# Graph layers on one core: angular nets in slot order, one product for keys and values, source gathers in place, and an earlier search of edges

## The chip, the core and the metric

The kernel runs on one core of a Trainium2 chip. The core has a matrix engine (PE, with its weight loads shown as PEld), a vector engine (DVE), an activation engine (ACT), a general engine (POOL, which here mostly issues gathers and scatters) and SyncE (SP, which issues transfers). The metric is the device time of one execution in microseconds (us), lower is better.

## The reference

A graph of 6250 nodes (128 features) and 206,250 edges, sorted by destination, goes through two layers, each followed by a residual add and a layer norm.

```python
# layer 1: five rounds of normalized neighbour sums, then a product
for _ in range(K):                                   # K = 5
    h = segment_sum(h[col] * w[:, None], row, num_segments=N)
    x_out = x_out + coef * h
y1 = x_out @ weight.T + bias
...
# layer 2: attention over the edges of each destination
def _conv_per_edge(x_src, edge_attr, edge_sh, Wang, Wlin, W1, b1, W2):
    rad = relu(edge_attr @ W1 + b1) @ W2
    g = edge_sh @ Wang.T
    return x_src * g @ Wlin * rad
x_src = node_attr[src]
k = _conv_per_edge(x_src, ..., Wang_k, Wlin_k, W1k, b1k, W2k)    # 64 wide
v = _conv_per_edge(x_src, ..., Wang_v, Wlin_v, W1v, b1v, W2v)    # 128 wide
alpha = einsum('ehq,qk,ehk->eh', q[dst], Wdot, k)                # 8 heads
attn  = softmax of alpha over the edges of one destination
out   = segment_sum(attn[..., None] * v, dst) @ Wout
```

The change is about `x_src * g` for keys and values together, about `relu(edge_attr @ W1 + b1)`, and about the lists of sources and edge attributes that both need.

## The kernel before

The nodes are cut into 49 tiles of 128. Everything runs in three stages.

**The count stage** (`count_rows`) writes `counts`, a matrix that says how often each node is a source of each other node. For tile `t`, `hot` makes two one-hot tables on DVE (L223), `count` multiplies them on PE (L357) and ACT evicts them (L361), and `put` transposes on DVE (L370, L375) and stores from SP. Tiles come in chunks of 7 (the first two chunks are 2 and 5). For each chunk, `look_at` gathers destinations on POOL (L274); `find_of` counts on DVE where each node's edges begin (L283), makes the positions (L288), and gathers the sources `src_e` on POOL (L290, 7 gathers of 128 rows); `split` on DVE takes the sources apart (L311, L313 to L318) for the tables of the chunk. The loop over `t` writes out by hand where each of these stands: in the old text `find_of` and the next `look_at` come when `t + 2 == a - 3`, `split` when `t + 2 == a - 1`, where `a` is the chunk's first tile. PE, DVE, ACT and POOL run in the order written here.

**The propagation** (`propagate`) does the five rounds as dense products. Each round has four quarters of destinations; in each, for 49 source tiles, SP loads `counts`, DVE (L600) and ACT (L605 to L613) cast it, and PE multiplies (L617). After each step over a source tile, `next(side, None)` runs one step of a side job: first `order_nodes`, which ranks the nodes by degree, then `lay_edges`, which lays the edges of each ranked tile out in slots. A tile has as many slots as `WIDTHS` says (64 down to 22, 1658 in all); slot `j` of a tile holds the `j`-th edge of each of its 128 nodes. `lay_edges` goes by pieces of up to 16 slots, five side steps apart. For a piece, `gather` gathers its edge attributes `ea_l` on POOL (L816), and with the first piece of a tile all the tile's sources into `src_all` (L812); two pieces later ACT splits off an upper part (L823), then DVE takes the rest (L827), then DVE transposes both parts into `eT_l`, a ring of 4 buffers (L835), and POOL stores both to `eas_o` (L841). PE, DVE and ACT run in the order written; POOL's order in this stage is chosen by a scheduler.

**The attention stage** (`attend`) goes through the slots in 433 groups of up to 4 (397 have 4). `fetch` gathers on POOL the source's features, one gather a slot (L961), into 6 buffers, and has SP load the edge attributes `ea` as four blocks `b` of 32 edges, each with its slots side by side. In iteration `i` PE runs `nets(i)` (three products of 512 columns, L1005: one for the radial net's first layer into `p_h`, two for keys and values into the two banks of `p_g`), `radial(i - 1)` (L1024), `turn(i + 1)` (transposes of the gathered features, L991) and `keys(i - 1)` (L1038, L1040). ACT makes the relu (L1007), evicts `p_r` (L1028) and the transposes (L994). DVE multiplies the features with both angular nets into `mkv` (L1013, two products a group), then keys and values with the radial part (L1045 to L1049), and between these takes steps of the softmax of the tile before (L1074 to L1121; the long ones are L1090, L1094 and L1097).

In `nets` the columns of a product are ordered (block, slot, edge), since that is how `ea` lies in memory; `r1`, `mkv` and the features are ordered (slot, block, edge), so L1007 and L1013 reorder as they read and write.

Of the kernel before, what the change touches and what calls it, by code (L numbers as in the profile page):

```python
# [12 lines left out]
AF = mybir.ActivationFunctionType  # L13
OP = mybir.AluOpType
# [4 lines left out]
P = 128  # L19
# [24 lines left out]
SC = 16  # L44
# [183 lines left out]
def count_rows(tc, row, first, cnt, dinv, hs, srct, dstt, tab_lo, tab_hi, iota, ident, ident_b,  # L228
# [10 lines left out]
    nc = tc.nc  # L239
    with tc.tile_pool(name="cr1", bufs=1) as one, tc.tile_pool(name="cr2", bufs=2) as two, \  # L240
# [8 lines left out]
        at = one.tile([P, NT], I32, name="at_e")  # L249
# [52 lines left out]
        def scale(t0, t1):  # L302
            for t in range(t0, t1):
                nc.scalar.mul(hs[:, t], hs[:, t], dinv[:, t:t + 1])
# [3 lines left out]
        def split(a, b):  # L308

            x, n = slice(a, b), b - a  # L310
            nc.vector.tensor_tensor(ok[:, :n], iota[:, None, :SLOTS].to_broadcast([P, n, SLOTS]),  # L311
                                    cnt[:, x, None].to_broadcast([P, n, SLOTS]), OP.is_lt)
            nc.vector.tensor_single_scalar(low[:, :n], src[:, x], 63, OP.bitwise_and)  # L313
            nc.vector.tensor_single_scalar(high[:, :n], src[:, x], 6, OP.logical_shift_right)
            nc.vector.tensor_copy(lh[:, x, 0:2], low[:, :n, None, :].to_broadcast([P, n, 2, SLOTS]))

            for i in (2, 3):
                nc.vector.scalar_tensor_tensor(lh[:, x, i], ok[:, :n], -float(P), high[:, :n],  # L318
                                               op0=OP.mult, op1=OP.add)

        def turn(t):

            p_t = pt.tile([P, 2, P], BF, name="p_lh")
            for i in range(2):
                nc.tensor.transpose(p_t[:, i, :], lh[:, t, 2 * i:2 * i + 2].rearrange("p a j -> p (a j)"),
                                    ident_b)
            turned[t] = two.tile([P, 2, 64], BF, name="lhT")
            for a in range(2):
                y = slice(64 * a, 64 * a + 64)
                nc.scalar.copy(turned[t][y], p_t[y, :, y])  # L330

        def hot(t):

            v = turned.pop(t)
            oh_lo = two.tile([P, 64 // Q, 64, Q], BF, name="oh_l")
            one_hot(nc, oh_lo, v[:, 0, :], tab_lo, 64)
            oh_hi = two.tile([P, 64 // Q, 4 * H4, Q], BF, name="oh_h")
            one_hot(nc, oh_hi, v[:, 1, :], tab_hi, 4 * H4)
            return oh_lo, oh_hi
# [61 lines left out]
        def look_at(i):  # L401
            if i < len(chunks):
                look(ends[i], ends[i + 1])

        def find_of(i):
            find(ends[i], ends[i + 1], *chunks[i])

        with tc.manual_schedule(engines=MANUAL | {mybir.EngineType.Pool}):
            look_at(0)
            find_of(0)  # L410
            look_at(1)
            split(*chunks[0])
            hots = {}
            for t in range(-2, NT + 1):
                for i, (a, b) in enumerate(chunks[2:]):
                    if t + 2 == a - 3:
                        find_of(i + 2)
                        look_at(i + 3)
                    if t + 2 == a - 1:
                        split(a, b)  # L420
                if t == 0:
                    hots[1] = hot(1)
                    split(*chunks[1])
                if 0 <= t + 2 < NT:
                    turn(t + 2)
                if 0 <= t + 1 < NT and t != 0:
                    hots[t + 1] = hot(t + 1)
                if t == -1:
                    find_of(1)
                    look_at(2)  # L430
                if 0 <= t < NT:
                    count(t, *hots.pop(t))
                    next(more, None)
                if 0 <= t - 1 < NT:
                    put(t - 1)
                if t == NT - 9:
                    nc.vector.tensor_scalar(dinv, cnt, 1.0, None, OP.add)
                    nc.scalar.activation(dinv, dinv, AF.Sqrt)
                    nc.vector.reciprocal(dinv, dinv)
                if t >= NT - 8:  # L440
                    scale(min(6 * (t - NT + 8), NT), min(6 * (t - NT + 9), NT))
# [358 lines left out]
def lay_edges(tc, one, ring, rows, srct, eat, src_all, eas_o):  # L800

    nc = tc.nc
    at = one.tile([P, WIDTHS[0] // SC, NT], I32, name="at_l")
    for c in range(WIDTHS[0] // SC):
        nc.vector.tensor_scalar(at[:, c], rows[:, :, 1], float(c * SC), None, OP.add)

    def gather(t, c, s, n):  # L810
        if c == 0:
            nc.gpsimd.indirect_dma_start(  # L812
                out=src_all[:, OFFS[t]:OFFS[t + 1]], out_offset=None, in_=srct[:, :],
                in_offset=bass.IndirectOffsetOnAxis(ap=at[:, 0, t:t + 1], axis=0))
        e = ring.tile([P, SC * 32], F32, name="ea_l", bufs=6)[:, :n * 32]
        nc.gpsimd.indirect_dma_start(  # L816
            out=e, out_offset=None, in_=eat[:, :],
            in_offset=bass.IndirectOffsetOnAxis(ap=at[:, c, t:t + 1], axis=0))
        return n, s, e

    def split(n, s, e):
        upper = ring.tile([P, SC * 32], FR, name="up_l", bufs=3)[:, :n * 32]
        nc.scalar.copy(upper, e)  # L823
        return n, s, e, upper

    def rest(n, s, e, upper):
        nc.vector.tensor_sub(e, e, upper)  # L827
        return n, s, e, upper

    def turn(n, s, e, upper):  # L830

        ys = []
        for x in (upper.bitcast(F32), e):
            y = ring.tile([P, SC * 32], F32, name="eT_l", bufs=4)[:, :n * 32]
            nc.vector.transpose(y, x)  # L835
            ys.append(y)
        return n, s, ys

    def put(n, s, ys):
        for i, y in enumerate(ys):  # L840
            nc.gpsimd.dma_start(  # L841
                bass.AP(tensor=eas_o.tensor, offset=eas_o.offset + (i * 32 * OFFS[NT] + s) * P,
                        ap=[[n * 32, 4], [OFFS[NT] * P, 32], [1, n * 32]]), y)

    todo = [(t,) + p for t in range(NT) for p in pieces(t)]
    got = {}
    for p in range(len(todo) + 5):
        for f, late in ((put, 5), (turn, 4), (rest, 3), (split, 2), (gather, 0)):
            if 0 <= p - late < len(todo):
                got[p - late] = f(*(got[p - late] if late else todo[p]))  # L850
        for _ in range(5):
            yield


def pieces(t):

    return [(c, OFFS[t] + c * SC, min(SC, WIDTHS[t] - c * SC)) for c in range(-(-WIDTHS[t] // SC))]
# [30 lines left out]
def attend(tc, w1, b1, wang, w2, wlin, wqd, wout, ident, rows, c_iota, src_all, eas_o, x1_d, x1_r, out):  # L888


    nc = tc.nc
    WM = WIDTHS[0]
    with ExitStack() as s:
# [9 lines left out]
        b1_s = one.tile([P, 1], F32, name="b1_s")  # L903
# [4 lines left out]
        with tc.tile_pool(name="at_w", bufs=1) as pool:  # L908
            wz = pool.tile([P, 2 * D], F32, name="wz")
            nc.vector.memset(wz, 0.0)  # L910
            for src, dst, at in ((w1, w1_s, 0), (wang, wang_s, 64)):
                n = src.shape[1]
# [19 lines left out]
        ea, kv, qw, x1s, keep, ok, al = {}, {}, {}, {}, {}, {}, {}  # L932
        xs, xT, r1, mkv, rr = {}, {}, {}, {}, {}
# [62 lines left out]
        def nets(g):  # L996

            t, j, n = groups[g]

            p_h = pp.tile([P, CH], F32, name="p_h")  # L1000
            p_g = pp.tile([P, 2, CH], F32, name="p_g")
            i = j % SC
            e = ea[t, j // SC][:, :, i * 32:(i + n) * 32]
            for o, wt in ((p_h, w1_s), (p_g[:, 0], wang_s[:, :D]), (p_g[:, 1], wang_s[:, D:])):
                nc.tensor.matmul(o[:, :n * P], wt, e, start=True, stop=True)  # L1005
            r1[g] = two.tile([P, 4, P], F32, name="r1")
            nc.scalar.activation(r1[g][:, :n].rearrange("p j (b e) -> p b j e", b=4),  # L1007
                                 p_h[:, :n * P].rearrange("p (b j e) -> p b j e", b=4, e=32),
                                 AF.Relu, bias=b1_s)
            mkv[g] = two.tile([P, 2, 4, P], F32, name="mkv")  # L1010
            x = xT.pop(g)[:, :n].rearrange("p j (b e) -> p b j e", b=4)
            for i in range(2):
                nc.vector.tensor_tensor(  # L1013
                    mkv[g][:, i, :n].rearrange("p j (b e) -> p b j e", b=4),
                    p_g[:, i, :n * P].rearrange("p (b j e) -> p b j e", b=4, e=32), x, OP.mult)

        def radial(g):

# [114 lines left out]
        with tc.manual_schedule(engines=MANUAL):  # L1133
            for i in range(-3, len(groups) + 1):
# [11 lines left out]
                if live[0]:  # L1146
                    keys(i - 1)
                    t, j, n = groups[i - 1]
# [162 lines left out]
def gnn_kernel(ctx, tc, x, srcf, dstx, srcp, dstp, easT, eas, wT0, b0, wq, wdot, w1, b1,  # L1311
# [40 lines left out]
    with ExitStack() as s:  # L1352
# [44 lines left out]
        def loads():  # L1397
# [5 lines left out]
            for e in range(0, EP, SUP * CH):  # L1403
                yield
                nc.scalar.dma_start(eat[e:e + SUP * CH], eas[e:e + SUP * CH], cond=unsorted < 1)

        count_rows(tc, row, first, cnt, dinv, hs, srct, dstt, tab_lo, tab_hi, iota, ident,
                   ident_b, counts, loads())

# [101 lines left out]
```

## Time and profile before

| what | us |
|---|---|
| median of 3 runs (4299.01 to 4313.89) | 4309.51 |
| the profiled execution, its own time | 4312.55 |
| its span, first to last instruction | 4310.8 |
| PE busy in the span | 3753.0 (87%) |
| DVE busy | 3492.5 (81%) |
| POOL busy | 2418.2 (56%) |
| ACT busy | 2052.8 (48%) |
| window 65 to 505 us (count): PE, DVE, POOL busy | 357, 401, 132 |
| window 525 to 2060 us (propagation): PE, DVE, POOL busy | 1450, 1100, 539 |
| window 2060 to 4311 us (attention): PE, DVE, POOL busy | 1938, 1961, 1718 |

A line of a group names the source line, the engine, the operation, output and input tiles, the count, then the busy time and the mean duration of one in ns, then the idle time of the engine just before these instructions with what ended it. In a timeline a line begins with its start and its duration in us, and the bracket at its end is the idle time before it. A wait line reads: who waited for whom, the total in us, how many times, and the longest. Shares over the whole span mix three stages with different limits, so stages are read one by one.

### The profile page before, as it was taken

The numbers are of one execution on the slowest core, as the hardware profiler recorded it, in microseconds if no ns is written. First come the engines' busy times: TensorE is split into PE (matmuls) and PEld (weight loads), VectorE is DVE, ScalarE is ACT, GpSimd is POOL, SyncE is SP. The second block draws the span as 40 slices with busy tenths as digits, with TensorE's granted clock in tenths as the row PEclk, the third lists the DMA queues.
The fourth block names the chain that finished last, engine by engine and source line by source line (L and its number), as shares of the span: only waits on it lengthen the run. The fifth ranks groups of instructions, "written<-read, shape, count | busy, mean of one in ns | idle before, by whom it ended". The sixth has DMA issues, their size and how long they took to land.

```text
span 4310.8 us, 76970 instructions
## 1 busy us (share of the span) xinstructions
PE 3753.0 (87%) x26392; PEld 3321.9 (77%) x26392; DVE 3492.5 (81%) x6175; ACT 2052.8 (48%) x4187; POOL 2418.2 (56%) x2388
## 2 busy tenths in 40 slices
PE   4877799799999999997788888888888888888883
PEld 3777688587878888875778888788888788887883
DVE  5999795587777877665598889998889989989995
ACT  3777754464654655543334444444434443444441
POOL 4233006633334433122777777777777777777776
PEclk8676699899999999998899999999999999999996
DMA  3776556699988998563655555556555655654551
GB/s 109 200 192 172 130 143 155 158 235 224 230 205 214 246 237 227 155 165 99 122 100 99 107 100 100 105 97 106 98 99 104 111 100 98 108 103 95 102 106 44
DMA packets 394939, 603.48 MB, mean 140 GB/s; under 512 B 124669, under 2 KB 329781, under 8 KB 383658
## 3 DMA queue, kind: packets, MB, share of 16 engines
q1 hardware_dynamic: 259552, 355.34, 38.2%
q0 software_dynamic: 128624, 207.89, 21.5%
q10 hardware_dynamic: 6362, 35.22, 2.6%
q8 instruction: 214, 3.51, 0.4%
q14 instruction: 187, 1.53, 0.1%
HBM read 493.45 MB, written 132.25 MB: 145 GB/s over the span
## 4 chain that ended last, share of the span: by engine, by line
PE 47%; DVE 18%; DMA 14%; issue 10%; POOL 9%; ACT 2%; SPq 1%; DVEq 0%; ACTq 0%; POOLq 0%
PE acc L617 23%; DMA xs<-x_d,src_all 7%; PE p_r L1024 6%; PE p_k L1040 5%; POOL xs L961 5%; PE p_k L1038 4%; DVE mkv L1013 4%; DMA c<-counts 3%; DVE kv L1045 3%; PE p_c L357 3%; PE p_g L1005 2%; DVE oh_h L223 2%; DVE kv L1090 2%; PE p_x L991 2%; DVE kv L1097 1%
## 5 line engine op out<-in xcount | busy, mean ns | idle before, releaser
L961 POOL DMA_INDIRECT xs<-x_d,src_all x1658 | 1674.9, 1010 | 507.1 <-issue 419.7
L617 PE MATMUL acc<-c,parts 128*128 128x512 f32 (+1 forms) x6370 | 1420.8, 383 | 69.6 <-DVE c L600 49.7
L617 PEld LDWEIGHTS acc<-c,parts 128*128 128x128 f32 x6370 | 1154.7, 189 | 306.1 <-DVE c L600 65.9
L600 DVE CAST c<-c 128x1024 fp32r<-128x1024 uint8 x980 | 679.4, 715 | 282.2 <-PE acc L617 157.2
L1040 PE MATMUL p_k<-wlin_s,mkv 128*128 128x128 f32 x3316 | 750.8, 309 | 0.0
L613 ACT CAST c<-c 128x512 fp32r<-128x512 uint8 x735 | 451.9, 623 | 582.1 <-PE acc L617 376.8
L1038 PE MATMUL p_k<-wlin_s,mkv 128*128 128x64 f32 x3316 | 579.7, 257 | 64.1 <-DVE kv L1045 62.3
L1024 PE MATMUL p_r<-w_s,r 128*128 128x192 f32 x3316 | 617.3, 329 | 0.0
L1038 PEld LDWEIGHTS p_k<-wlin_s,mkv 128*128 128x128 f32 x3316 | 520.6, 198 | 95.5 <-DVE kv L1045 94.8
L1024 PEld LDWEIGHTS p_r<-w_s,r 128*128 128x128 f32 x3316 | 567.5, 193 | 33.4 <-ACT rr L1028 0.2
L1028 ACT COPY rr<-p_r 128x768 f32<-128x768 f32 (+2 forms) x443 | 335.3, 759 | 475.1 <-PE p_r L1024 459.7
L1013 DVE TENSOR_TENSOR mkv<-p_g,xT 128x512 f32<-128x512 f32 (+3 forms) x866 | 534.2, 659 | 6.3 <-PE p_g L1005 6.2
L1045 DVE TENSOR_TENSOR kv<-rr,p_k 128x768 f32<-128x768 f32 (+2 forms) x443 | 397.0, 898 | 154.7 <-PE p_k L1040 139.3
L1040 PEld LDWEIGHTS p_k<-wlin_s,mkv 128*128 128x128 f32 x3316 | 520.2, 198 | 0.0
L1007 ACT ACTIVATE r<-p_h,b_s 128x512 f32<-128x512 f32 (+3 forms) x433 | 290.6, 671 | 453.2 <-PE p_h L1005 443.4
L841 POOL DMA_DIRECT2D eas_o<-eT_l x252 | 205.5, 818 | 526.1 <-DVE eT_l L835 517.6
L357 PE MATMUL p_c<-oh_h,oh_l 64*64 64x100 bf16 x6272 | 340.9, 271 | 44.5 <-DVE oh_h L223 36.7
L357 PEld LDWEIGHTS <-oh_l 64*64 64x64 bf16 x6272 | 329.4, 141 | 53.2 <-DVE oh_h L223 41.6
L991 PE MATMUL p_x<-ident,xs 128*128 128x128 f32 x1658 | 274.9, 278 | 86.0 <-DMA xs<-x_d,src_all 79.1
L361 ACT CAST cT<-p_c 128x500 uint8<-128x500 f32 (+1 forms) x637 | 307.3, 648 | 33.2 <-DVE c_row L375 23.5
L991 PEld LDWEIGHTS p_x<-ident,xs 128*128 128x128 f32 x1658 | 212.3, 142 | 116.5 <-DMA xs<-x_d,src_all 98.4
L1005 PE MATMUL p_g<-ea,wang_s 128*128 128x512 f32 (+3 forms) x866 | 282.1, 408 | 15.9 <-DVE mkv L1013 13.0
(216 smaller groups left out, 4171.3 us busy)
## 6 DMA issues: line engine op xcount, KB each, us to landing
c<-counts SPq DMA_DIRECT2D x720, 192.0 KB
ea<-eas_o SPq DMA_DIRECT2D x648, 128.0 KB
c<-counts SPq DMA_DIRECT2D x240, 224.0 KB
eas_o<-eT_l POOLq DMA_DIRECT2D x162, 256.0 KB
counts<-c_row SPq DMA_DIRECT2D x196, 144.0 KB
xs<-x_d,src_all POOLq DMA_INDIRECT x1658
eat<-in_eas ACTq DMA_DIRECT2D x31, 832.0 KB
counts<-c_row SPq DMA_DIRECT2D x196, 56.0 KB
```

The source lines that it names most:

```text
L357: nc.tensor.matmul(p_cs[k][y, q % 5], oh_lo[y, q // Q, :, q % Q], oh_hi[y, q // Q, :, q % Q], start=True, stop=True)
L600: nc.vector.tensor_copy(c[:, u:u + 1024].rearrange("p (n b x) -> p n b x", n=2, b=2), r[:, :, v:v + 512].rearrange("p b (n x) -> p n b x", ...
L613: nc.scalar.copy(c[:, 1024:w].rearrange("p (b x) -> p b x", b=2), r[:, :, 512:])
L617: nc.tensor.matmul(a[:, :v - u], parts[:, j, i, :], c[:, u:v], start=(j == 0 and i == 0), stop=(j == NT - 1 and i == 1))
L961: fetched = nc.gpsimd.indirect_dma_start(out=xs[g][:, i, :], out_offset=None, in_=x1_d[:, :], in_offset=bass.IndirectOffsetOnAxis(ap=src_a ...
L991: nc.tensor.transpose(p_x[:, i * P:(i + 1) * P], xs[g][:, i, :], ident)
L1005: nc.tensor.matmul(o[:, :n * P], wt, e, start=True, stop=True)
L1013: nc.vector.tensor_tensor(mkv[g][:, i, :n].rearrange("p j (b e) -> p b j e", b=4), p_g[:, i, :n * P].rearrange("p (b j e) -> p b j e", b=4 ...
L1024: nc.tensor.matmul(p_r[:, i // 2, u:u + DK + D], r[:, i, :], w2_s, start=True, stop=True)
L1038: nc.tensor.matmul(p_k[:, i // 2, u:u + DK], m[:, 0, i, :], wlin_s[:, :DK], start=True, stop=True)
L1040: nc.tensor.matmul(p_k[:, i // 2, u + DK:u + DK + D], m[:, 1, i, :], wlin_s[:, DK:], start=True, stop=True)
L1045: nc.vector.tensor_mul(k.rearrange("p (b i) f -> p b (i f)", b=b.stop - b.start), r2[:, b, :f], p_k[:, b, :f])
```

## The change

Three places change.

1. In the count stage, the search of the next chunk's edges (`find_of`) and the look at the chunk behind it (`look_at`) are issued one tile earlier; `split` stays.
2. In `lay_edges`, the gather of a tile's sources is kept in the order in which the program issues it, before the tile's first gather of attributes. Before, the scheduler placed it: from the third tile on, the gathers of all sources stood in one row around the first stores to `eas_o`.
3. In `nets`, PE reads the edge attributes slot by slot (runs of 32 elements, ordered slot, block, edge), so `p_h` and `p_g` are in slot order. The relu then reads and writes straight, and one DVE product over both banks of `p_g`, with the features repeated, takes the place of two.

```diff
-                    if t + 2 == a - 3:
+                    if t + 2 == a - 4:
                         find_of(i + 2)
                         look_at(i + 3)
...
-            nc.gpsimd.indirect_dma_start(
+            tc.keep_in_program_order(nc.gpsimd.indirect_dma_start(
                 out=src_all[:, OFFS[t]:OFFS[t + 1]], out_offset=None, in_=srct[:, :],
-                in_offset=bass.IndirectOffsetOnAxis(ap=at[:, 0, t:t + 1], axis=0))
+                in_offset=bass.IndirectOffsetOnAxis(ap=at[:, 0, t:t + 1], axis=0)))
...
-            e = ea[t, j // SC][:, :, i * 32:(i + n) * 32]
+            e = ea[t, j // SC][:, :, i * 32:(i + n) * 32].rearrange("p b (j e) -> p j b e", e=32)
...
-            nc.scalar.activation(r1[g][:, :n].rearrange("p j (b e) -> p b j e", b=4),
-                                 p_h[:, :n * P].rearrange("p (b j e) -> p b j e", b=4, e=32),
-                                 AF.Relu, bias=b1_s)
+            nc.scalar.activation(r1[g][:, :n].rearrange("p j e -> p (j e)"), p_h[:, :n * P], AF.Relu,
+                                 bias=b1_s)
             mkv[g] = two.tile([P, 2, 4, P], F32, name="mkv")
-            x = xT.pop(g)[:, :n].rearrange("p j (b e) -> p b j e", b=4)
-            for i in range(2):
-                nc.vector.tensor_tensor(
-                    mkv[g][:, i, :n].rearrange("p j (b e) -> p b j e", b=4),
-                    p_g[:, i, :n * P].rearrange("p (b j e) -> p b j e", b=4, e=32), x, OP.mult)
+            x = xT.pop(g)[:, :n].rearrange("p j e -> p (j e)")
+            nc.vector.tensor_tensor(mkv[g][:, :, :n].rearrange("p i j e -> p i (j e)"), p_g[:, :, :n * P],
+                                    x[:, None].to_broadcast([P, 2, n * P]), OP.mult)
```

## The prediction

> **What bounds the kernel now.** I read the page first (span, slices), then the busy times by stage, then in each stage the waits, and the timeline only where a wait was long. Three stages follow one another: the count (to about 505 us), the propagation (525 to 2047 us) and the attention stage (from the first L961 gather, at 2047.9 us, to the end).
>
> The attention stage is the longest. The page, its POOL row (slices of 107.8 us) and the costliest group:
>
> ```profile
> span 4310.8 us, 76970 instructions
> ...
> POOL 4233006633334433122777777777777777777776
> ...
> L961 POOL DMA_INDIRECT xs<-x_d,src_all x1658 | 1674.9, 1010 | 507.1 <-issue 419.7 <-DMA xs<-x_d,src_all 37.5 <-PE p_x L991 24.5
> ```
>
> A gather of 1.01 us and an idle 0.31 us make 1.316 us, and 1658 of them fill 2047.9 to 4228.6 us without a gap. The waits of POOL between 2100 and 4200 us, then the busy time there:
>
> ```profile
> POOL xs L961 <- issue: 403.3, 1323, 0.3
> ```
> ```profile
> 2600.00:3100.00 500.00, 443.37 (x3014) 405.42 (x3014) 449.12 (x780) 204.86 (x343) 384.48 (x380) 0.97 0.55 101
> ```
>
> The longest idle time is 0.3 us: POOL never pauses, while PE (443 of 500 us) and DVE (449) have a tenth to spare. So in this stage the gather queue sets the pace: 4 slots of a group cost it 5.26 us. A shorter PE or DVE helps only where it shortens a gather.
>
> In the propagation PE is the bound, 69 to 70 of 71 us, but one quarter is not like the others. The last quarter of round 0, then the same quarter of rounds 1 and 3 (columns: time, PE, PEld, DVE, ACT, POOL, PE clock, DMA share, GB/s):
>
> ```profile
> 738.30:841.00 102.70, 74.18 (x310) 59.83 (x309) 51.64 (x83) 36.77 (x68) 72.70 (x73) 0.85 0.64 148
> 1057.60:1128.60 71.00, 69.43 (x308) 56.02 (x308) 52.86 (x89) 34.65 (x70) 26.60 (x30) 1.00 0.90 221
> 1634.70:1706.40 71.70, 69.82 (x308) 56.09 (x307) 53.85 (x91) 37.07 (x73) 22.47 (x27) 1.00 0.84 224
> ```
>
> The same work takes 31.3 us longer than the mean of the other two (71.35). The timeline of that quarter says why:
>
> ```profile
> 796.89 0.95 POOL L812 DMA_INDIRECT src_all<-srct,at_l  x1 [0.30 <-issue]
> 797.83 1.51 POOL L841 DMA_DIRECT2D eas_o<-eT_l  x2
> ...
> 805.17 0.71 DVE L835 STREAM_TRANSPOSE eT_l<-up_l 128x512 f32<-128x512 f32 x1 [23.23 <-DMA eas_o<-eT_l]
> 808.25 0.71 DVE L835 STREAM_TRANSPOSE eT_l<-ea_l 128x512 f32<-128x512 f32 x1 [2.38 <-DMA eas_o<-eT_l]
> ```
>
> DVE's third pair of transposes needs the buffers that the first `eas_o` put has to empty. That put stands on POOL behind a row of `src_all` gathers; DVE waits 23.2 us, its casts for PE are queued behind the transpose, and PE idles.
>
> In the count stage DVE is the bound (401 of 440 us between 65 and 505), a plain tile taking 7.7 us. Once in seven tiles it waits at L313 for the sources that L290 gathers, which started about two tiles earlier:
>
> ```profile
> 98.98 0.40 DVE L313 TENSOR_SCALAR low_e<-src_e 128x448 int32<-128x448 int32 x1 [1.63 <-DMA src_e<-srct,at_e]
> 163.41 0.41 DVE L313 TENSOR_SCALAR low_e<-src_e 128x448 int32<-128x448 int32 x1 [4.39 <-issue]
> 227.92 0.40 DVE L313 TENSOR_SCALAR low_e<-src_e 128x448 int32<-128x448 int32 x1 [4.52 <-issue]
> 292.06 0.63 DVE L313 TENSOR_SCALAR low_e<-src_e 128x448 int32<-128x448 int32 x1 [4.17 <-DMA dst_g<-dstt,row_i]
> 357.98 0.39 DVE L313 TENSOR_SCALAR low_e<-src_e 128x448 int32<-128x448 int32 x1 [5.71 <-DMA dst_g<-dstt,row_i]
> 419.58 0.40 DVE L313 TENSOR_SCALAR low_e<-src_e 128x448 int32<-128x448 int32 x1 [1.36 <-issue]
> ```
>
> **The search a tile sooner.** These six waits sum to 21.8 us. L313 runs 18.3 to 22.4 us after the first L290 gather of its chunk (142.4 to 163.4 us for the second). DVE is ready 16.6 us after it (L311 starts at 158.39 us and takes 0.62); a tile more makes 24.3, over the largest need by 1.9 us, so all six should go. What moves: per chunk, 7 L283 counts with two short DVE steps, a small product, 7 L290 and 7 L274 gathers. The DVE work is the same and only stands a tile earlier; POOL is busy 132 of 440 us here and its queue holds nothing else in these tiles. The first of these chunks has its L274 rows only just issued (the last at 67.84 us, landing some 1.7 us after its 0.95, as the first L274 row did), so its search ends near 72.5 and the one-hot tables queued behind it start 2 us later than their 70.4; the 2.2 us that the same search took at 78.2 are saved for that. Net nothing. As the margin is small I take 21 us; the bounds are 0 (the sources are late whatever the start) and 21.8.
>
> **The gathers in place.** In the built order 47 of the 49 `src_all` gathers leave the row around the first puts and stand one per tile before that tile's first `ea_l` gather (the first two stood so already). The count of DMAs is the same, and the queues of SP and ACT are untouched. Worth: the quarter falls from 102.7 to 71.35, so 31 us; bounds 23.5 (the longest PE wait alone) and 34.1 (all that DVE waits for `eas_o` there). The moved gathers cost POOL 47 x 1.26 = 59 us, hidden in the 511 us that it waits at L841 for DVE's transposes between 840 and 1725 us. Without that cover, puts would be late by up to 1.26 us a tile, and behind them DVE's transposes and casts. The last source now arrives near 1680 us, still far ahead of the first L961 gather.
>
> **The nets slot by slot.** The three 512-column products read `ea` in runs of 32 instead of 128; L1007 writes straight; two L1013 products of 512 become one of 1024, 433 DVE instructions fewer. The trace has no such product. Nearest rows: L1013 itself, 681, 549, 416 and 282 ns for 512, 384, 256 and 128 elements, 1.04 ns each; so 1024 take 681 + 531 = 1.21 us, and L1045, which also reads two PSUM banks at once, lies on the same slope (950 ns for 768). The old pair starts 0.597 us apart, 1.194 in all; the new one should take 0.597 + 0.531 = 1.128 before the next can start: 0.066 us saved, 26 us over the 397 full groups. But POOL is the bound. DVE shortens the stage only where its own loop holds gathers up: in the fullest groups (a 1024-element L1090 and L1094 in one) DVE runs back to back at 5.37 us a group, and each time one gather takes 1.22 us instead of 0.95 while L1094 runs. Those are at most 180 groups (the L1094 rows of all sizes): 12 us. Bounds 0 and 12 from this, 26 if DVE paced everything; I take 6. Waiting for both halves of `p_g` costs nothing: L1013 idles 6.3 us in the whole run.
>
> [...]
>
> **Sum.** The profiled execution took 4312.55 us (span 4310.8 and 1.75 around it). Less 21, 31 and 6 it is 4254.5. The median of the runs shown is 3.0 lower (4309.51), so I forecast 4252 us, own range 4239 to 4266.
>
> **The rivals.**
> *DVE paces the attention after all.* For it: the 5.37 us groups. Against: no POOL pause over 0.3 us. All 26 us would show: 4232.
> *A late transfer stays late.* The sources land after 24.3 us because the copies of `eat` crowd the same DMA engines (busy 65% in this stage), or puts still hold DVE in round 0. Half of 21 + 31 kept: 4278; if only one of the two is halved, 4263 to 4268.
> *The long product holds up gathers (slower).* I paired each L961 gather with the DVE row running 0.2 us after its start: beside L1090, the only 1024-element product with a broadcast operand, it took 0.35 us longer (181 cases); beside L1013 (404 cases, at 0.6 us) 0.03. The new product is 1024 long with a broadcast operand. If it acts as L1090 does, 433 x 0.35 = 152 us fall on the queue that bounds the stage: 4258 + 152 = 4410. It makes the kernel slower from 0.15 us a product. Against it: L1090 reads both operands from SBUF, L1013 and L1045 (0.04) one from PSUM, and the new one does too.
> [...]
> *PE reads slower in runs of 32.* The products start 0.23 us apart when back to back; doubled, that is 0.69 us a group, 299 us on a PE with 314 idle in 2251. It would then meet POOL's pace, and I estimate 60 us more for the groups where PE is already the slower one: 4258 + 60 = 4318. Against: L357 reads its moving operand with a step of 4 elements, its 100 columns 0.055 us apart at a clock of 0.68.
> *The change does not act.* The scheduler could hold the old order; the built order shows the new one. 4309.
>
> **How the numbers follow.** Forecast 0.60, DVE 0.13, late transfers 0.15, held gathers 0.06, slow reads 0.03, no effect 0.03. A difference under 0.3% (13 us, about what the three runs differ by) can't be told from none. Faster than 4296.5: the first three, 0.88. Within: 0.05, the no-effect case and half of the slow reads. Slower: 0.07. The range takes in the forecast, the DVE case and most of the late transfers: 4229 to 4275.
>
> **What would show it.** Right: L313 without a wait over 1 us after 90 us; the last quarter of round 0 in 70 to 73 us with no PE gap; L1013 433 times, about 1.21 us; L961 still about 1.31 us apart, with no pause. Wrong: a DVE wait on `eas_o` that comes back later in the propagation, gathers longer than 1.05 us in the mean, or L1005 matmuls longer than their 0.42 and 0.49 us.

## The result and the profile after

The changed kernel took 4243.73 us in the median of 4 runs (4236.67 to 4250.39), the kernel before 4311.70 us beside it (4299.01 to 4319.74). The ratio is 0.9845, with a 95% interval from 0.9815 to 0.9875: 1.5% faster. The profiled execution of the changed kernel took 4246.2 us, with a span of 4244.4.

Where the span's 66.4 us went, stage by stage, from the starts of the first L617 product and of the first feature gather (L961 before, L962 after) and the start of the last gather:

| stretch | before | after | difference |
|---|---|---|---|
| start to first L617 (count) | 523.9 | 504.6 | -19.3 |
| last quarter of round 0 | 102.8 | 68.9 | -33.9 |
| the rest, first L617 to first feature gather | 1421.2 | 1430.1 | +8.9 |
| first to last feature gather | 2180.7 | 2161.7 | -19.0 |
| last gather to the end | 82.2 | 79.2 | -3.0 |

The +8.9 of the third row is scatter for the most part: rounds 1 to 4 take between 1171.0 and 1184.4 us in the kernels of this document, whichever parts of the change they have. Before they took 1176.3 us and after 1184.0, but 1174.0 in the kernel with the gathers in place alone.

The page of the changed kernel, its POOL row (slices of 106.1 us) and the group of the gathers:

```profile
span 4244.4 us, 76210 instructions
...
POOL 5443005444444442113777777777777777777776
...
L962 POOL DMA_INDIRECT xs<-x_d,src_all x1658 | 1655.4, 998 | 507.5 <-issue 417.6
```

The row still stands at 7 from the start of the attention stage to its end, and a gather takes 998 ns where it took 1010. The waits of POOL between 2100 and 4200 us, and below them the busy time of the same kernel between 2600 and 3100 us:

```profile
POOL xs L962 <- issue: 398.4, 1307, 0.3
```
```profile
2600.00:3100.00 500.00, 446.02 (x3025) 411.19 (x3025) 445.31 (x687) 204.65 (x345) 383.84 (x382) 0.96 0.56 102
```

No pause is longer than 0.3 us: the gather queue still sets the pace, and it has 382 gathers in 500 us where it had 380. The nets' own groups (line, engine, operation, tiles, count, then busy us and mean ns):

```profile
L1013 DVE TENSOR_TENSOR mkv<-p_g,xT 128x1024 f32<-128x1024 f32 (+3 forms) x433 | 506.3, 1169 | 5.7 <-PE p_g L1007 4.5
...
L1007 PE MATMUL p_g<-ea,wang_s 128*128 128x512 f32 (+3 forms) x866 | 282.5, 408 | 11.1 <-DVE mkv L1013 10.5
```

The last quarter of round 0 (time, PE, PEld, DVE, ACT, POOL, PE clock, DMA share, GB/s), and DVE's wait for `eas_o` in the whole run (total us, times, longest), both of the changed kernel:

```profile
718.50:787.40 68.90, 68.90 (x310) 56.62 (x309) 51.32 (x84) 37.64 (x71) 27.77 (x28) 1.00 0.84 216
```
```profile
DVE eT_l L836 <- DMA eas_o<-eT_l: 4.4, 2, 3.9
```

PE is busy in all of the 68.9 us, and POOL does 28 instructions there where it did 73. The wait of 23.2 us is gone and has not come back elsewhere: the longest is 3.9. The timeline of L313 in the count stage, second to fourth chunk:

```profile
95.25 0.38 DVE L313 TENSOR_SCALAR low_e<-src_e 128x448 int32<-128x448 int32 x1
158.85 0.38 DVE L313 TENSOR_SCALAR low_e<-src_e 128x448 int32<-128x448 int32 x1
218.95 0.39 DVE L313 TENSOR_SCALAR low_e<-src_e 128x448 int32<-128x448 int32 x1
```

None has a bracket with an idle time. After 90 us DVE no longer waits for sources at all.

### The profile page after: what moved, and what is told of

The parts are those of the page before. It is cut to its first block, busy times and chain, and to the rows that moved or that the text cites. A ratio compares the mean times of both kernels' runs of the same rounds, so it can differ in the third digit from the quotient of the medians.

```text
span 4244.4 us, 76210 instructions
## 1 busy us (share of the span) xinstructions
PE 3742.1 (88%) x26392; PEld 3325.0 (78%) x26392; DVE 3464.7 (82%) x5742; ACT 2047.3 (48%) x4187; POOL 2435.1 (57%) x2388
## 4 chain that ended last, share of the span: by engine, by line
PE 49%; DVE 19%; DMA 14%; issue 8%; POOL 6%; SPq 1%; ACT 1%; DVEq 0%; ACTq 0%; POOLq 0%
PE acc L617 26%; DMA xs<-x_d,src_all 7%; PE p_r L1023 6%; PE p_k L1039 5%; POOL xs L962 4%; DMA c<-counts 4%; DVE kv L1044 4%; DVE mkv L1013 4%; PE p_k L1037 4%; PE p_g L1007 2%; DVE kv L1089 2%; DVE oh_h L223 2%; PE p_c L357 2%; PE p_x L992 2%; DMA counts<-c_row 1%
## 5 line engine op out<-in xcount | busy, mean ns | idle before, releaser
L962 POOL DMA_INDIRECT xs<-x_d,src_all x1658 | 1655.4, 998 | 507.5 <-issue 417.6
L617 PE MATMUL acc<-c,parts 128*128 128x512 f32 (+1 forms) x6370 | 1417.4, 382 | 46.4 <-DVE c L600 26.1
L617 PEld LDWEIGHTS acc<-c,parts 128*128 128x128 f32 x6370 | 1152.2, 189 | 281.7 <-DVE c L600 42.2
L1037 PE MATMUL p_k<-wlin_s,mkv 128*128 128x64 f32 x3316 | 580.3, 258 | 71.0 <-DVE kv L1044 70.0
L1037 PEld LDWEIGHTS p_k<-wlin_s,mkv 128*128 128x128 f32 x3316 | 520.4, 198 | 102.9 <-DVE kv L1044 102.1
L1044 DVE TENSOR_TENSOR kv<-rr,p_k 128x768 f32<-128x768 f32 (+2 forms) x443 | 396.6, 897 | 164.8 <-PE p_k L1039 146.5
L1013 DVE TENSOR_TENSOR mkv<-p_g,xT 128x1024 f32<-128x1024 f32 (+3 forms) x433 | 506.3, 1169 | 5.7 <-PE p_g L1007 4.5
L842 POOL DMA_DIRECT2D eas_o<-eT_l x252 | 207.0, 825 | 495.7 <-DVE eT_l L836 453.3
```

The lines of the kernel that those rows point to most:

```text
L617: nc.tensor.matmul(a[:, :v - u], parts[:, j, i, :], c[:, u:v], start=(j == 0 and i == 0), stop=(j == NT - 1 and i == 1))
L962: fetched = nc.gpsimd.indirect_dma_start(out=xs[g][:, i, :], out_offset=None, in_=x1_d[:, :], in_offset=bass.IndirectOffsetOnAxis(ap=src_a ...
L1013: nc.vector.tensor_tensor(mkv[g][:, :, :n].rearrange("p i j e -> p i (j e)"), p_g[:, :, :n * P], x[:, None].to_broadcast([P, 2, n * P]), O ...
L1037: nc.tensor.matmul(p_k[:, i // 2, u:u + DK], m[:, 0, i, :], wlin_s[:, :DK], start=True, stop=True)
L1044: nc.vector.tensor_mul(k.rearrange("p (b i) f -> p b (i f)", b=b.stop - b.start), r2[:, b, :f], p_k[:, b, :f])
```

## The experiments

**Each part alone, and the change without its nets.** Three kernels are the one before with one part of the change; the fourth is the changed one with the old `nets`. The edits are hunks of the diff above: the first for the search, the second for the gathers in place, the third for the nets.

```diff
# search alone
-                    if t + 2 == a - 3:
+                    if t + 2 == a - 4:
# place alone
-            nc.gpsimd.indirect_dma_start(
+            tc.keep_in_program_order(nc.gpsimd.indirect_dma_start(
```

> The kernel before with only the search a tile sooner. Theory (the sources land in time): DVE's six waits at L313 after 90 us, 21.8 us in sum, go; the propagation's first L617 product starts about 19 us sooner, as it does with the whole change (523.9 to 504.6 us); time 20 us under the kernel before, ratio 0.995. Rival (transfers crowded by the copies of eat stay late): half of the waits stay, ratio 0.9975 or more.

> The kernel before with only the source gathers in place. Theory (the puts stood behind the row of gathers): the last quarter of round 0 falls from 102.7 to 69 to 72 us, nothing of it comes back, time 31 us under the kernel before, ratio 0.993. Rival (the moved gathers cost something in the later rounds, where the whole change lost some 8 us against before): quarter as in the theory, but rounds 1 to 4 together 8 us longer than the 1176.3 us of before, ratio 0.995.

> The kernel before with only the nets slot by slot and one product. Theory as predicted (POOL sets the pace, DVE's saving counts only in the fullest groups): first to last gather of the attention stage 6 us shorter than the 2180.7 us of before, 12 at most. Rival (DVE's saving of 0.066 us a group comes through in nearly every group): 19 to 26 us shorter, as the whole change showed (2161.7 us), ratio about 0.995.

> The whole change without the nets (search and place). Theory (the parts add up): ratio 0.988, some 52 us under the kernel before; the attention stage's gathers as before, 2180 us from first to last and 1.01 us each. Rival (the shorter gathers of the whole change have another cause than the nets, such as the time at which the stage starts): gathers 0.998 us here too, first to last near 2162 us, ratio 0.9845 as the whole change.

Measured, with 95% intervals of the ratio to the kernel before, and from each profile the stage that the part touches:

| kernel | ratio | first L617 | last quarter, round 0 | gathers, first to last |
|---|---|---|---|---|
| before | 1 | 523.9 | 102.8 | 2180.7 |
| search alone | 0.9942 [0.9924, 0.9960] | 503.6 | 103.0 | 2180.2 |
| place alone | 0.9927 [0.9908, 0.9947] | 525.3 | 68.9 | 2174.1 |
| nets alone | 0.9968 [0.9958, 0.9979] | 524.8 | 102.2 | 2162.6 |
| search and place | 0.9862 [0.9846, 0.9878] | 504.7 | 68.9 | 2182.7 |

Each part changes its own stage; in the other columns a kernel differs from the ones like it by at most 2 us, and by 9 us in the gathers. The parts add up: of 4316 us the three ratios are 25, 32 and 14 us, 70 in all, against 67 for the whole change. The column of the gathers puts the nets at 16 to 20 us in their stage (2174.1 to 2182.7 with the old nets, 2161.7 and 2162.6 with the new, one profiled execution each): about three times the 6 of the prediction.

**Is it the merging, or the straight order?** The changed kernel with two straight products of 512 in place of one of 1024.

```diff
-            nc.vector.tensor_tensor(mkv[g][:, :, :n]..., p_g[:, :, :n * P],
-                                    x[:, None].to_broadcast([P, 2, n * P]), OP.mult)
+            for i in range(2):
+                nc.vector.tensor_tensor(mkv[g][:, i, :n]..., p_g[:, i, :n * P], x, OP.mult)
```

> The changed kernel with the slot order kept, but two straight products of 512 in the place of one of 1024. Theory (the saving is the second instruction's fixed part): the pair again starts 0.597 us apart, 1.19 in all, and the gathers of the attention stage take 2175 to 2183 us from first to last, as without the nets. Rival (the straight reading does it): a shorter pitch than 0.597 and 2162 us, as with the one product.

The ratio is 0.9841 [0.9825, 0.9858], which cannot be told from the changed kernel. Its profile can: the stage takes 2175.3 us, 13.6 more than with one product, and lies among the kernels with the old nets; two products start 0.598 us apart, as the old ones did. So in the stage the gain is the merging, as far as single profiled executions tell it (this one, 4258.61 us, was the slowest of four; their median is 4249.40). The run time does not resolve it.

**What holds the gathers.** The changed kernel with its two long DVE instructions of the softmax (the weighting L1089 and the sum L1093) replaced by reductions over the same elements, which read one operand from SBUF instead of two. The weighting and most of the sum are left out.

```diff
-                nc.vector.tensor_tensor(av, av, ex[:, u:u + k, :, None].to_broadcast(...), OP.mult)
+                nc.vector.tensor_reduce(m...[:, :k], a[:, u:u + k, DK:], AX.X, OP.max)
...
-                    nc.vector.tensor_add(a[:, :k, DK:], a[:, :k, DK:], a[:, u:u + k, DK:])
+                    nc.vector.tensor_reduce(m...[:, :k], a[:, u:u + k, DK:], AX.X, OP.max)
```

> The changed kernel with the softmax's two long products of 1024 (the weights times the values, and the sum over blocks of slots) replaced by reductions over the same 1024 elements into a small tile; so the weights and most of the sum are left out. DVE's time stays about the same, but these instructions read one SBUF operand instead of two. Theory (a DVE instruction with two SBUF operands holds up a gather that starts beside it): gathers fall from 0.998 to 0.965 us in the mean or less, first to last from 2161.7 to 2110 us or less. Rival (gathers are held by DVE's pace, whatever its operands): both stay within 10 us.

The ratio is 0.9686 [0.9666, 0.9706]. The gathers of this kernel, from its groups:

```profile
L962 POOL DMA_INDIRECT xs<-x_d,src_all x1658 | 1596.7, 963 | 512.2 <-issue 423.7 <-DMA xs<-x_d,src_all 31.9 <-PE p_x L992 20.6
...
L1089 DVE TENSOR_REDUCE m<-kv 128x8 f32<-128x1024 f32 (+6 forms) x229 | 251.8, 1100 | 0.3
```

A gather takes 963 ns for 998, and the stage 2107.7 us for 2161.7, while the DVE instruction takes 1100 ns as before (1107). So it is not DVE's time that gathers lose to. The reduction also writes less (8 elements for 1024), but the nets' product writes 1024 and holds no gather, as the count below shows; what is left is what the instruction reads. The timeline of the changed kernel shows one such meeting (start, duration, engine, line):

```profile
2301.92 0.95 POOL L962 DMA_INDIRECT xs<-x_d,src_all  x1 [0.30 <-issue]
...
2302.91 1.22 DVE L1089 TENSOR_TENSOR kv<-kv,ex 128x1024 f32<-128x1024 f32 x1
...
2303.18 1.77 POOL L962 DMA_INDIRECT xs<-x_d,src_all  x1 [0.30 <-issue]
```

and the same meeting in the kernel with reductions:

```profile
2180.05 1.21 DVE L1089 TENSOR_REDUCE m<-kv 128x8 f32<-128x1024 f32 x1
...
2180.24 0.95 POOL L962 DMA_INDIRECT xs<-x_d,src_all  x1 [0.30 <-PE p_k L1039]
```

In the first the DVE instruction ends at 2304.13 and the gather at 2304.95, 0.82 us later. So it is nearly throughout the trace. Of the changed kernel's 1658 gathers 450 take over 0.02 us longer than the free 0.952; set beside the DVE rows, 444 of these end 0.805 to 0.845 us after the end of a DVE product, sum or difference with both operands in SBUF (L1089 174 of them, L1046 192, the rest at other lines), none after L1013 or L1044, which read one operand from PSUM. The 174 beside L1089 start between 0.01 us before it and 1.05 us into it, and all end 0.818 to 0.832 us after its end: in these the end of the gather follows the end of the instruction, not the gather's own start. With the reductions, none of the 195 gathers that start while L1089 runs is held.

**What a longer DVE loop costs.** The changed kernel with one more DVE instruction a group, a memset of 256 elements into a tile that nobody reads.

```diff
+            nc.vector.memset(extra, 0.0)
```

> The changed kernel with one more DVE instruction a group: a memset of 256 elements of a tile that nothing reads, about 0.24 us, no SBUF operand. As predicted (DVE's time shows only in the fullest groups, at most 180 of 433): first to last gather 20 to 43 us longer than 2161.7. Rival (two thirds of DVE's time shows, as with the nets, which saved 18 of 28 us): about 70 us longer. If DVE paced every group: 104 us. If POOL alone set the pace: none.

Its groups show the instruction and the gathers:

```profile
L963 POOL DMA_INDIRECT xs<-x_d,src_all x1658 | 1703.5, 1027 | 506.7 <-issue 434.3 <-DMA xs<-x_d,src_all 28.6 <-PE p_g L1008 15.8
...
L1016 DVE MEMSET extra<- 128x256 f32 x433 | 117.8, 272 | 0.7
```

The memset costs the loop 0.274 us a group where 0.24 was expected. The stage grew by 47.3 us (2161.7 to 2209.0), the ratio is 0.9941 [0.9925, 0.9958]. That is 40% of the 118 us that DVE had more to do: a little above the range expected where POOL is the bound, far under what a DVE bound would give. All of it is longer gathers (1703.5 - 1655.4 = 48.1 us), not pauses between them. The memset pushes the weighting later against the gather that the weighting holds: in the fullest groups the weighting starts 1.405 us after L1013 for 1.131, the gather stays 2.015 us after L1013, and the hold grows in the median from 0.204 to 0.418 us.

**Is it the late put that held round 0?** The kernel before with six buffers for `eT_l` instead of four, all else as it was.

```diff
-            y = ring.tile([P, SC * 32], F32, name="eT_l", bufs=4)[:, :n * 32]
+            y = ring.tile([P, SC * 32], F32, name="eT_l", bufs=6)[:, :n * 32]
```

> The kernel before with a ring of 6 buffers for the transposed attributes instead of 4, POOL's order as before. Theory (DVE waits for a buffer that the late put has to empty): the first pair of transposes to wait is one piece later, and pieces are 7.2 us apart, so the longest wait falls from 23.2 to about 16 us and the last quarter of round 0 from 102.7 to about 95. Rival (it is the late gathers of attributes that hold the side job): no change, 102.7.

```profile
DVE eT_l L835 <- DMA eas_o<-eT_l: 28.7, 4, 17.2
```

The wait on `eas_o` falls from 23.2 to 17.2 us at its longest, and the quarter from 102.8 to 97.7 us. This is one execution, and it took 4311.71 us against 4314.94 before. More buffers move the wait by about one piece (7.2 us) and do not remove it, as it should be if the first put is late on POOL's queue; with late gathers of attributes, the rival, the quarter would not have changed.

**Two versions that might be faster still, and the changed kernel again.** The first cuts the long products into pieces of four slots. The second keeps them long, but lets ACT copy the softmax weights into spare columns of the PSUM banks of `p_r` and `p_k`, so that L1089 (L1098 there) reads one operand from PSUM. Both compute the whole result.

```diff
# halves
+                for b in range(0, k, 4):
+                    c = slice(u + b, u + min(b + 4, k))
...
# weights in PSUM
+            for q in range(-(-w // SC)):
+                f = min(SC, w - q * SC) * H
+                nc.scalar.copy(part(q)[:, :f], ex[:, q * SC:q * SC + f // H]...)
...
-                nc.vector.tensor_tensor(av, av, ex[:, u:u + k, :, None].to_broadcast(...), OP.mult)
+                nc.vector.tensor_tensor(av, av, xp[:, :, :, None].to_broadcast(...), OP.mult)
```

> The changed kernel with each long softmax product (L1089, eight slots) and each long sum (L1093) issued as instructions of at most four slots; the same numbers are computed. Theory A (the hold that a gather suffers is set by the length of the one DVE instruction with two SBUF operands that runs when it starts): each hold falls by about half, the L962 mean from 0.998 to about 0.985 us, which is 22 us of the stage; about 409 more DVE instructions, each 0.062 us more start-up by the slope of L1013, cost 25 us of DVE, of which 40% (the share that the longer-DVE run showed) is 10 us. Net 12 us less than the changed kernel: stage about 2150 us, time about 4232 us. Theory B (the hold depends on the sum of DVE time with two SBUF operands, however it is cut): the L962 mean stays at 0.998 us, the stage takes 2162 to 2172 us, time 4244 to 4254 us.

> The changed kernel with the softmax weights copied by ACT into the 128 spare columns of the PSUM banks of p_r and p_k, so that the long product L1089 reads one operand from SBUF and one from PSUM; the same numbers are computed. Theory A (two SBUF operands are what holds a gather): the 178 gathers beside L1089 lose their excess of 0.275 us, 49 us in all, the L962 mean falls from 0.998 to about 0.97 us and the stage from 2161.7 to between 2113 and 2140 us: time 4195 to 4222 us. L1093, which keeps two SBUF operands, still holds its gathers by about 0.17 us. Theory B (what holds a gather is the long product itself, its broadcast or its length, wherever the operand lies): L962 stays at 0.998 us and the stage takes 2162 us or more: time 4244 us or more. Theory C (the holds go, but the copies on ACT and the shared banks bring new waits of PE on p_r or p_k): L962 falls as in A, the pitch of gathers does not, and pauses of POOL over 0.3 us appear.

> The changed kernel once more, unaltered, because the two runs before fell on a chip on which the kernel before itself took 4884 us. On a chip where the kernel before takes 4300 to 4325 us: about 0.9845 of it. On a chip like the last one, where gathers wait for PE (POOL waiting over 200 us for p_x transposes): if the search and place parts (52 us together) are worth the same there and the nets nothing, (4884 - 52)/4884 = 0.989; if the nets help PE's loop too, below that.

> The halves again, beside the changed kernel on one chip: the expectation is the one given for it before. Theory A (hold set by the length of one instruction): 12 us less than the changed kernel, L962 mean 0.985 us. Theory B (hold set by the DVE time with two SBUF operands, however it is cut): 0 to 10 us more than the changed kernel, L962 mean 0.998 to 1.000 us; the last run showed 1.000 us, but with gathers that waited for PE as well.

These four runs were on a chip on which the kernel before took 4884.24 and 4886.06 us, 13% more than on the others, so only their ratios and their like stages are compared.

| kernel | median us | ratio to before | L962 mean ns | gathers, first to last |
|---|---|---|---|---|
| the changed kernel again | 4804.49 | 0.9830 [0.9798, 0.9863] | 1015 | 2619.7 |
| halves, first run | 4813.39 | 0.9863 [0.9835, 0.9890] | 1000 | 2615.3 |
| halves, second run | 4810.45 | 0.9862 [0.9830, 0.9893] | 1002 | 2596.9 |
| weights in PSUM | 5550.09 | 1.1374 [1.1345, 1.1404] | 971 | 3344.9 |

The change itself is worth the same share there, and more than the 0.989 expected if the nets were worth nothing on that chip. The halves shorten the mean gather by 13 to 15 ns, 21 to 24 us over 1658 gathers, as theory A says. One of them, with the two halves of a product in one line (x2, the first of them 0.68 us long):

```profile
2244.37 1.28 DVE L1091 TENSOR_TENSOR kv<-kv,ex 128x512 f32<-128x512 f32 x2
2244.45 1.43 POOL L962 DMA_INDIRECT xs<-x_d,src_all  x1 [0.30 <-issue]
```

The gather ends at 2245.88, 0.825 us after the first half, while the second runs until 2245.65. So it is with every held gather that meets a first half (120 in the first run, 117 in the second): none waits for the second, which speaks against theory B. But the mean hold beside the weighting falls from 0.443 to 0.32 us, not by half. The time did not follow; that the gathers are not the only bound on this chip is the likely reason, but was not tested. The waits of POOL in the changed kernel there, between 2100 and 4600 us (`remote` is a release that the profile puts on no instruction):

```profile
POOL xs L962 <- issue: 407.8, 1330, 1.1
POOL xs L962 <- PE p_x L992: 230.2, 95, 6.5
POOL xs L962 <- remote: 116.0, 62, 5.1
```

POOL now waits for PE up to 6.5 us at a time. Whether the halves would be faster on a chip like the others was not tried.

With the weights in PSUM the hold beside the product is gone. Its timeline:

```profile
2472.21 1.22 DVE L1098 TENSOR_TENSOR kv<-kv,p_r 128x1024 f32<-128x1024 f32 x1 [3.21 <-ACT rr L1033]
...
2472.41 0.95 POOL L969 DMA_INDIRECT xs<-x_d,src_all  x1 [3.85 <-PE p_x L999]
```

None of the 58 gathers that start while L1098 runs is held, although it is the same product, as long and with the same broadcast; beside the sum, which still reads two operands from SBUF, 25 of 28 are. That is theory A against theory B. But the sharing of the banks costs far more than it saves. The waits of POOL and of PE in that kernel (PE over its whole run, POOL between 2100 and 5400 us):

```profile
POOL xs L969 <- PE p_x L999: 1233.6, 301, 10.2
```
```profile
PE p_r L1029 <- DVE kv L1098: 506.2, 141, 5.1
PE p_r L1029 <- ACT p_r L1091: 203.6, 40, 9.1
```

PE may not write the next `p_r` until DVE has read the weights out of its bank, and the gathers stand behind PE: theory C. No version run here that computes the whole result was faster than the changed kernel beyond the intervals.

## Why the prediction was right, point by point

**The bound and the sum.** The prediction's 4254.5 us for the profiled execution stand against 4246.2. The three terms were 21, 31 and 6; the stages show 19.3 (20.3 alone), 33.9 (33.9 alone) and 19.0 (18.1 alone) with 3.0 more behind the last gather. That the sum came within 8.3 us is in part luck: these stages gave 75.2 us where 58 were forecast, and the 8.9 us of scatter in the propagation took half of the surplus back.

**The search** went as worked out. All waits for sources after 90 us are gone, and the distance is the one forecast: the L290 gathers that begin at 134.57 us are read by L313 at 158.85, 24.3 us later. The one-hot tables of the first tiles lost nothing that was not saved again: the first L617 is 19.2 to 20.3 us sooner.

**The gathers in place** went as worked out, and a little further: the quarter fell to 68.9 us, under the 71.35 taken from rounds 1 and 3. The mechanism is the late put (the ring of six), and the cover held: POOL's wait at L842 for DVE's transposes is 453.3 us in the changed kernel.

**The nets: the mechanism was right, the size was not.** The product came out as computed (1.215 us, and the next instruction starts 1.131 us after it; 1.21 and 1.128 were forecast), and POOL stayed the bound. The step that failed is "Bounds 0 and 12 from this, 26 if DVE paced everything; I take 6". Two things were wrong in it. First, halving: in the 130 fullest groups the held gather starts 2.02 us after L1013 in both kernels, so nothing that DVE saves ahead of the weighting is lost on the way. The weighting starts 1.195 us after L1013 before and 1.131 after, and the median hold falls from 0.267 to 0.204 us, by the whole 0.064. Second, the count and the line: the hold belongs to the weighting (L1090 before), not to L1094, and the weighting holds gathers in the other groups as well. By the line that held them:

| gathers held by | before: count, us | after: count, us |
|---|---|---|
| the weighting (L1090, L1089) | 179, 64.1 | 174, 48.8 |
| the sums (L1094 and L1097, L1093 and L1096) | 48, 12.2 | 49, 10.0 |
| the product with the queries (L1047, L1046) | 202, 14.6 | 192, 13.5 |
| all that gathers take over 0.952 us | 96.5 | 77.0 |

The 19.5 us of the last row are the stage's 19.0: an unhindered queue takes 1657 x (0.952 + 0.3055) = 2083.7 us, and with 77.0 of holds and 1.0 of pauses that makes the 2161.7. In the same way the 2209.0 of the longer DVE loop hold 125.1 of holds and 0.2 of pauses, and the 2107.7 of the reductions 18.3 and 5.7. This is bookkeeping: holds and pauses are read from the same trace, so the sum has to close, and it tells only where the time went. Over the kernel before and the experiments with the old nets on the first chips the holds are 88.0 to 96.5 us, 77.0 and 77.8 with the new ones, so the term is 10 to 20 us, 16 in the mean (93.2 over before, search, place and both, less 77.4), where 6 was taken.

So the stage has one bound with a surcharge. POOL's queue sets its pace; DVE adds to it, as far as these traces show, where an instruction with two SBUF operands meets a gather (444 of the 450 longer ones; 77.0 us are added in all), and what it adds ends with that instruction (the gather ends 0.805 to 0.845 us after it).

**The rivals.** *DVE paces everything* falls: 118 us more on DVE cost 47, and no pause appeared. *A late transfer stays late* falls with the two empty waits above. *The long product holds up gathers*: of the 400 gathers that start while the nets' product runs it holds none (five are longer, each by a later instruction with two SBUF operands), though it is as long as the weighting (1.215 us beside 1.22) and has a broadcast operand too; one of its operands lies in PSUM. *PE reads slower in runs of 32* falls: the 512-column products take 0.418 us for `p_g` and 0.498 for `p_h` (0.417 and 0.493 before), and back to back they start 0.231 us apart at the least (0.224 before), where the rival had them double.

What the prediction set against the held gathers, that the new product reads one operand from PSUM, is borne out on both sides: 174 gathers end about 0.825 us after the weighting, which reads both from SBUF; none of 195 is held beside the reduction, and none of 58 beside the weighting with an operand in PSUM. The nets' product holds none of the 400 beside it.

## What to carry to other kernels

When one queue sets the pace, write its stage as count times unhindered period plus the sum of what is added to single items, and look in the trace for which items those are: an engine that is not the bound can still charge the bound (77.0 of the 2161.7 us here), and its edits are then worth (items charged) x (time saved), not zero and not everything. If the item's place against the charging instruction is fixed, take the whole saving, not a half of it (the median hold here fell by the whole 0.064 us). And freeing the bound of a charge can cost more than it saves if it makes another engine wait for a buffer, as the weights in PSUM did (the mean gather fell to 971 ns, and the ratio was 1.1374).

## What the runs showed of the hardware that was not expected

Of the 450 longer gathers of the changed kernel 444 met a DVE product, sum or difference with both operands in SBUF, and these end about 0.825 us after that instruction, to within 0.02 us. Not every such meeting makes a gather longer: of the 392 that start with more than 0.15 us of L1089, L1046 or L1093 still to run, 15 took no longer than the free ones, and all 15 started within 0.04 us of the instruction's start. Beside the same product with an operand in PSUM (1.22 us) none of 58 gathers was held, and beside a reduction over the same 1024 elements (1.21 us) none of 195.

One chip took 13% more for the kernel before and the changed one alike. In the changed kernel there, POOL pauses 432 us in all between gathers (1.0 us elsewhere). Between 2100 and 4600 us PE, ACT and DVE stand idle together 66 times for more than 1 us, 236 us in sum; in the same kernel on the other chip they never do between 2100 and 4150 us. Of ACT's waits over 3 us there, the largest group ends in `remote` (64 of them). What it is stays open. After one such pause of PE (3.44 us, up to 2546.0) its granted clock was 0.50 for the next 4 us:

```profile
2536.00:2542.00 6.00, 5.05 (x38) 4.76 (x39) 3.05 (x7) 1.53 (x4) 4.62 (x5) 1.00 0.21 55
2546.00:2550.00 4.00, 3.98 (x19) 3.99 (x20) 0.53 (x2) 1.52 (x3) 1.99 (x3) 0.50 0.40 104
```

In these 4 us a pair of L1037 products took 0.53 us, where the pair at 2540.22 us had taken 0.33.
